# Second attention and routing of a two-layer decoder: one stage of eight units in place of two stages

## The chip, the cores and the metric

The kernel runs on one core of a Trainium2 chip. The metric is the time of one execution on the device in microseconds (us), median of several runs. Five engines work side by side, each through its own queue in order: TensorE (PE: matrix products and turns, with its weight loads shown apart as PEld), VectorE (DVE), ScalarE (ACT), GpSimd (POOL), and SyncE (SP), which here only issues transfers. Everything is in 32-bit floats.

## What is computed

The input has 8 rows of 512 positions with 256 channels. Two layers, each an attention and a feed-forward part, every part behind a normalization and added to its input. The first layer is an ordinary attention with relative positions, and a feed-forward part with GELU. The change touches the second layer:

```python
# attention over the eight ROWS at one position; 16 heads of 16 channels
qkv = x @ Wqkv.T + bqkv
scores = mask + scale * jnp.einsum('bnd,bmd->bnm', q, k)   # n, m: rows
out = softmax(scores) @ v ; x = x + out @ Wproj.T + bproj
# mixture of experts: 32 experts in 4 groups, 4 experts a token
scores = sigmoid(norm(x) @ router_weight.T); sfc = scores + router_bias
# keep the 2 best groups (sum of their two best), then the 4 best experts
x = x + sum_of_chosen(silu(t @ gate) * (t @ up) @ down * weight) + shared_expert(t)
```

The mask lets rows 0 to 3 see rows 0 to 3, and rows 4 to 7 see all eight rows. So the attention mixes rows, never positions: for each position a row has four or eight keys. The experts mix nothing; each token goes to four of them.

## The kernel before

The 4096 tokens are held in on-chip memory as x[0] to x[7], a row each, 128 partitions x 4 tiles x 256 channels (512 positions are 4 tiles of 128). The program has five stages: first attention, first feed-forward, second attention, routing, experts. Everything around the change is ordered by hand: inside `tc.manual_schedule()` the instructions stand in each engine's queue in the order in which the program makes them. No planner moves them.

**Second attention** (class `_L1Attention`, L723 to L985). Its weights come in early (`load`, during the feed-forward). Row 0 is measured and normalized at the end of the feed-forward (L698 to L702). For each row: `measure` and `norm` (DVE's statistics, a power on POOL at L57 for the root, a DVE shift at L751, four ACT instructions at L758), `turn` (8 turns on PE, L799, copies on ACT), `queries` (q and k, L812, evacuated with the bias on ACT, L815), `tokens` (v, L824). Rows 0 to 3 are prepared first; then the rest is prepared while rows 0 to 3 attend. Attention takes four query rows (a group g) at once:

- `multiplied` (L777): q of a row times k of a row, an elementwise product of 128 x 1024; 48 of them. `multiply` deals them to DVE, POOL, DVE in turn, by a counter.
- `summed` (L852): PE adds the channels of a head with a matrix of ones, four query rows beside each other in 32 columns each; `scored` (L869, L870) turns the sums to positions on the partitions.
- `softmax` (L880 to L887): maximum, difference, exponential on ACT (L882), sum, reciprocal, product.
- `weighted` (L777 again): v times its weights, 48 products of 128 x 1024, dealt out in the same way; `gathered` (L904): PE turns and adds them in PSUM; two ACT copies (L916); the bias added to x by POOL (L918).
- `projected` (L927, L935): PE multiplies by Wproj, DVE adds into x.

**Routing** (in `_l1_ffn`, L1083 to L1349), row by row, after the attention. Normalization (`measure`, `norm`), `turn` (L1105, L1108), `logits` (L1115, sigmoid L1119), `copies` (four ACT copies of the normalized rows into the payload, L1098), `hidden` and `gated` (the shared expert, L1266, L1268, L1274), `route` (some 50 small DVE instructions, L1125 to L1178, that choose 4 experts a token), `count`, `take` and `send` (L1184 to L1250: how many tokens each expert has so far, and from that a slot in a table of rows sorted by expert; room for each expert is rounded up to 128 rows). PE's small sums in `count`, `take` and `send` (L1184, L1197, L1198, L1219 to L1221) alternate with DVE's small instructions. Then 16 scatters a row (L1059, POOL, 128 rows of 264 numbers each) carry the payload to DRAM; `pace` issues them two at a time at fixed points of DVE's work, which the scatters wait for. `outputs` and `add_shared` (L1285, L1298) add the shared expert one row later. At the start of the routing SP loads its small weights (L1005 to L1028) and then the weights of all 32 experts in eight transfers of 1536 KB (L1031).

**Experts** (L1350 to L1480): 160 tiles of 128 sorted rows are fetched (`fetch`, after the last 16 scatters), turned, multiplied by their expert's weights (L1385, L1403), and scattered back by POOL (L1059, with the results). `gather`, `add`, `put` fetch the four results of a token, add them and write rows of the output.

A row's PSUM tiles come from pools: the attention's products of q, k, v and turns share two banks, and so do the routing's small sums.

Of the kernel before, what the change touches and what calls it, by code (L numbers as in the profile page):

```python
# [535 lines left out]
class _FFN:  # L536
# [99 lines left out]
    def run(self, rest, after):  # L636

        nc, tc, x, rows = self.nc, self.tc, self.x, self.rows
        with ExitStack() as ctx:
# [43 lines left out]
            with tc.manual_schedule():  # L683
# [5 lines left out]
                for b in range(B):  # L689
                    hT = sb.tile([P, NF, S], F32, tag="hT", name="hT")  # L690
                    for f in range(NF):
# [6 lines left out]
                        if b == B - 1:  # L698
                            if f == 2:
                                after.measure(0)  # L700
                            elif f == 4:
                                after.norm(0)  # L702
                            continue
# [19 lines left out]
class _L1Attention:  # L723

    SEEN = (4, 8)

    def __init__(self, nc, tc, a, x, ident, mhalf, wp):  # L730
        self.nc, self.tc, self.a, self.x, self.ident, self.mhalf, self.wp = nc, tc, a, x, ident, mhalf, wp
        self.stats, self.xl = {}, {}
# [14 lines left out]
    def measure(self, n):  # L747
        nc, wp = self.nc, self.wp
        mv, rstd = _batch_norm_stats(nc, wp, [self.x[n][:, t, :] for t in range(NT)], 1e-5, self.mhalf)
        shift = wp.tile([P, NT], F32, tag="shift", name="shift", bufs=2)  # L750
        nc.vector.scalar_tensor_tensor(shift, mv[:, :, 0], -1.0, rstd, ALU.mult, ALU.mult)  # L751
        self.stats[n] = rstd, shift

    def norm(self, n):
        rstd, shift = self.stats.pop(n)
        xl = self.xl[n] = self.wp.tile([P, NT, H], F32, tag="xl", name="xl", bufs=2)
        for t in range(NT):
            self.nc.scalar.activation(  # L758
                xl[:, t, :], self.x[n][:, t, :], AF.Identity, bias=shift[:, t : t + 1], scale=rstd[:, t : t + 1]
            )  # L760

    def run(self):
        nc, tc, x, ident = self.nc, self.tc, self.x, self.ident
        with ExitStack() as ctx:
            pool = lambda name, bufs, **kw: ctx.enter_context(tc.tile_pool(name=name, bufs=bufs, **kw))
            wp = pool("b_w", 1)
            sb = pool("b_sb", 2)
            ps_q = pool("b_psq", 2, space=PSUM)
            ps_s = pool("b_pss", 2, space=PSUM)
            ps_o = pool("b_pso", 2, space=PSUM)  # L770
            q, k, v = {}, {}, {}
            xlT, prods, sums, sc, values, turned = {}, {}, {}, {}, {}, {}
            engines = [nc.vector, nc.gpsimd, nc.vector]
            count = [0]

            def multiply(out, in0, in1):
                engines[count[0] % 3].tensor_tensor(out, in0, in1, ALU.mult)  # L777
                count[0] += 1

            def bank(name, pool=ps_q, tag="psq"):  # L780
                return pool.tile([P, S], F32, tag=tag, name=name)

            def biases():

                pb = bank("pb")
                for c in range(NK):
                    nc.tensor.matmul(
                        pb[:, :H], self.bcol[:, 4 + c : 5 + c].to_broadcast([P, P]), self.wproj[:, c, :],
                        start=c == 0, stop=c == NK - 1,
                    )  # L790
                nc.vector.tensor_tensor(self.bproj, self.bproj, pb[:, :H], ALU.add)


            def turn(n):
                xlT[n] = sb.tile([P, NK, S], F32, tag="xlT", name="xlT")
                for c in range(NK):
                    pt = bank("pt")
                    for t in range(NT):
                        nc.tensor.transpose(  # L799
                            pt[:, t * P : (t + 1) * P], self.xl[n][:, t, c * P : (c + 1) * P], ident  # L800
                        )
                    nc.scalar.copy(xlT[n][:, c, :], pt)

            def queries(n, c):

                to = (q, k)[c // NK]
                if c % NK == 0:
                    tag = f"q{n % 4}" if c < NK else f"k{n}"
                    to[n] = wp.tile([P, NK, S], F32, tag=tag, name=tag)
                pq = bank("pq")  # L810
                for i in range(NK):
                    nc.tensor.matmul(  # L812
                        pq, self.wqkv[:, i, c * P : (c + 1) * P], xlT[n][:, i, :], start=i == 0, stop=i == NK - 1
                    )
                nc.scalar.activation(to[n][:, c % NK, :], pq, AF.Identity, bias=self.bcol[:, c : c + 1])  # L815

            def tokens(n, half):
                if half == 0:
                    v[n] = wp.tile([P, NT, H], F32, tag=f"v{n}", name=f"v{n}")
                pv = bank("pv")  # L820
                for j in range(2):
                    t = 2 * half + j
                    for i in range(NK):
                        nc.tensor.matmul(  # L824
                            pv[:, j * H : (j + 1) * H],
                            xlT[n][:, i, t * P : (t + 1) * P],
                            self.wqkv[:, i, 2 * H :],
                            start=i == 0,
                            stop=i == NK - 1,
                        )  # L830
                nc.scalar.copy(v[n][:, 2 * half : 2 * half + 2, :].rearrange("p t c -> p (t c)"), pv)

            def row(n):
                ahead = [partial(self.measure, n + 1), partial(self.norm, n + 1)] if n + 1 < B else []
                steps = [partial(turn, n)]
                steps += [partial(queries, n, c) for c in range(4)] + [partial(tokens, n, h) for h in range(2)]
                for i, f in zip((2, 4), ahead):
                    steps.insert(i, f)
                return steps


            def multiplied(g, m):
                prods[g, m] = [sb.tile([P, NK, S], F32, tag="prod", name="prod", bufs=6) for r in range(4)]
                for r, p in enumerate(prods[g, m]):
                    multiply(p, q[4 * g + r], k[m])

            def summed(g, m):
                ps = bank("ps", ps_s, "pss")
                ends = prods.pop((g, m))
                for c in range(NK):  # L850
                    for r, p in enumerate(ends):
                        nc.tensor.matmul(  # L852
                            ps[32 * r : 32 * r + 32, :],
                            self.heads[:, c, :],
                            p[:, c, :],
                            start=c == 0,
                            stop=c == NK - 1,
                            skip_group_check=True,
                        )
# [105 lines left out]
            def beside(main, other):  # L965

                n, done = len(main), 0
                for i, f in enumerate(main):
                    f()
                    upto = (i + 1) * len(other) // n  # L970
                    for f in other[done:upto]:
                        f()
# [642 lines left out]
```

## Time and profile before

| | us |
|---|---|
| median of 3 runs | 2185.62 (2185.58 to 2187.22) |
| the profiled execution, its own time | 2187.77 |
| its span, first to last instruction | 2185.7 |
| first feed-forward ends, attention begins | 1403 |
| attention's last addition into x (L935) begins | 1680.9 |
| last scatter of the routing begins (L1059) | 1897.4 |
| first expert matmul (L1385) | 1904.1 |

Over the whole span PE is busy 2002.9 us (92%), DVE 1395.5 (64%), POOL 1213.7 (56%), ACT 1096.2 (50%), at a mean granted TensorE clock of 0.947. The first two stages hold PE at 90% and more. The rest is not so.

How to read the lines that follow. A line of the table of stretches gives the stretch (us from the span's start), its length, then for each engine its busy time and, after x, its instructions, then the TensorE clock that was granted as a share of full speed, the mean busy share of the DMA engines, and GB/s. A line of waits names the waiting engine, what it waited for with its line, the sum in us, how often, and the longest. A line of the groups has line, engine, operation, output <- inputs, shape, count | busy us in all, mean ns of one | idle time of the engine before them and what ended it. PE's matmuls are pipelined: their mean duration is longer than the busy time that each adds. A 32-bit product of two matrices stands as two instructions in PE's records.

### The profile page before, as it was taken

The numbers are of one execution on the slowest core, as the hardware profiler recorded it, in microseconds if no ns is written. First come the engines' busy times: TensorE is split into PE (matmuls) and PEld (weight loads), VectorE is DVE, ScalarE is ACT, GpSimd is POOL, SyncE is SP. The second block draws the span as 40 slices with busy tenths as digits, with TensorE's granted clock in tenths as the row PEclk, the third lists the DMA queues.
The fourth block names the chain that finished last, engine by engine and source line by source line (L and its number), as shares of the span: only waits on it lengthen the run. The fifth ranks groups of instructions, "written<-read, shape, count | busy, mean of one in ns | idle before, by whom it ended". The sixth has DMA issues, their size and how long they took to land. (4 is left out here: it accounts for less than half of the span.)

```text
span 2185.7 us, 46365 instructions
## 1 busy us (share of the span) xinstructions
PE 2002.9 (92%) x16100; PEld 1464.0 (67%) x16100; DVE 1395.5 (64%) x3664; ACT 1096.2 (50%) x2367; POOL 1213.7 (56%) x1367
## 2 busy tenths in 40 slices
PE   7999999999999999999998999977867888499997
PEld 4777777777777777777775666644536666388886
DVE  3676776767767667676666555344677767356666
ACT  2776676666666666666651222243211545044443
POOL 4666766767667676676753111032546467555554
PEclk7999999999999999999999999998989777699998
DMA  8998898888888988989873444900001622356887
GB/s 273 310 296 276 273 280 267 282 277 274 264 277 275 287 268 270 282 276 288 261 256 91 161 138 129 61 0 1 1 0 54 252 90 95 106 161 207 255 261 257
DMA packets 389061, 444.50 MB, mean 203 GB/s; under 512 B 43232, under 2 KB 368096, under 8 KB 388832
## 3 DMA queue, kind: packets, MB, share of 16 engines
q1 hardware_dynamic: 374048, 402.20, 60.8%
q0 software_dynamic: 13824, 38.29, 4.8%
q8 instruction: 132, 2.16, 0.4%
q10 hardware_dynamic: 960, 1.05, 0.1%
q14 instruction: 97, 0.79, 0.1%
HBM read 239.26 MB, written 202.19 MB: 202 GB/s over the span
## 5 line engine op out<-in xcount | busy, mean ns | idle before, releaser
L389 DVE CUSTOM_DVE_ANT_0 e<-sc,winc 128x512 f32<-128x512 f32 x512 | 333.2, 688 | 297.9 <-PE sc L375 132.5
L391 ACT ACTIVATE e<-e,low 128x512 f32<-128x512 f32 x512 | 365.8, 716 | 115.5 <-DVE low L389 110.4
L316 POOL TENSOR_TENSOR own<-aside,strip 128x512 f32<-128x512 f32 x256 | 268.5, 1049 | 217.2 <-ACT strip L313 200.9
L313 ACT COPY strip<-pa 128x512 f32<-128x512 f32 x512 | 275.3, 591 | 209.0 <-issue 80.1
L363 PE MATMUL sc<-sm,sm 32*128 32x256 f32 (+3 forms) x1792 | 321.3, 438 | 16.7 <-DVE low L389 16.7
L400 DVE COPY et<-et_ps 128x512 f32<-128x512 f32 x512 | 328.5, 683 | 0.2 <-PE et_ps L398 0.2
L306 PE MATMUL pa<-pos,sm 32*128 32x256 f32 x2048 | 299.9, 406 | 1.7 <-ACT sm L290 1.0
L398 PE MATMUL et_ps<-ident,e 128*128 128x128 f32 x2048 | 267.4, 274 | 0.2 <-DVE et L400 0.2
L363 PEld LDWEIGHTS sc<-sm,sm 32*128 32x128 f32 x1792 | 161.8, 184 | 126.3 <-issue 49.4
L398 PEld LDWEIGHTS et_ps<-ident,e 128*128 128x128 f32 x2048 | 233.4, 142 | 0.6 <-ACT e L391 0.5
L343 POOL TENSOR_TENSOR winp<-winp,own 128x256 f32<-128x256 f32 x256 | 186.5, 729 | 74.9 <-DMA winp<-shift 63.5
L1059 POOL DMA_INDIRECT results<-y,r x160 | 156.0, 975 | 124.3 <-ACT y L1405 100.1
L375 PE MATMUL sc<-ident,winp 128*128 128x128 f32 x1280 | 200.1, 285 | 7.9 <-DMA winp<-shift 7.8
L343 POOL TENSOR_TENSOR winc<-winc,own 128x256 f32<-128x256 f32 x256 | 186.7, 729 | 33.8 <-DMA winc<-shift 28.4
L57 POOL TENSOR_TENSOR rstd<-var,mhalf 128x4 f32<-128x4 f32 x40 | 40.8, 1019 | 292.1 <-DVE var L55 267.4
L375 PEld LDWEIGHTS sc<-ident,winp 128*128 128x128 f32 x1280 | 136.4, 141 | 83.1 <-issue 62.6
L306 PEld LDWEIGHTS pa<-pos,sm 32*128 32x128 f32 x2048 | 180.3, 187 | 13.7 <-ACT strip L313 3.6
L1385 PE MATMUL pge<-store,rT 128*128 x640 | 167.9, 385 | 3.0 <-DVE rT L1379 2.8
L1059 POOL DMA_INDIRECT rows<-pay,slot x128 | 128.0, 1000 | 75.2 <-issue 23.8
L410 PE MATMUL ctx_ps<-et,v 128*16 128x128 f32 x4096 | 137.6, 274 | 0.2 <-DVE et L400 0.2
L282 PE MATMUL pq<-xnT,wqk 128*128 128x512 f32 x256 | 127.0, 617 | 4.3 <-DVE xnT L77 4.3
L660 ACT ACTIVATE hT<-ph,b 128x512 f32<-128x512 f32 x64 | 43.9, 687 | 170.0 <-PE ph L657 170.0
(219 smaller groups left out, 3530.8 us busy)
## 6 DMA issues: line engine op xcount, KB each, us to landing
shift<-strip SPq DMA_DIRECT2D x256, 510.0 KB
winp<-shift SPq DMA_DIRECT2D x128, 384.0 KB
winc<-shift SPq DMA_DIRECT2D x128, 384.0 KB
winp<-shift SPq DMA_DIRECT2D x128, 256.0 KB
winc<-shift SPq DMA_DIRECT2D x128, 256.0 KB
rows<-empty SPq DMA_DIRECT2D x8, 2640.0 KB
r<-rows SPq DMA_DIRECT2D x160, 132.0 KB
z<-results SPq DMA_DIRECT2D x32, 512.0 KB
```

What stands on the lines that cost most here:

```text
L306: nc.tensor.matmul(pa[:, t * W : (t + 1) * W], src[rs, i * P : (i + 1) * P], pos[rs, g, :], start=True, stop=True)
L313: nc.scalar.copy(st[:, 2 * j : 2 * j + 2, :].rearrange("p t w -> p (t w)"), pas[j])
L316: nc.gpsimd.tensor_tensor(own, aside.unsqueeze(2).to_broadcast([P, 2, 2, P]), st[:, :, W - 1 : W].rearrange("p (j t) o -> p t j o", t=2).t ...
L343: nc.gpsimd.tensor_tensor(dst, dst, own[:, t], ALU.add)
L363: nc.tensor.matmul(sc[:, c0:c1], s[side_][rs, cut : cut + P], s[2 + side_][rs, c0:c1], start=c0 == 0, stop=False, skip_group_check=True,)
L375: nc.tensor.matmul(sc[:, m * P : (m + 1) * P], wins[n + 2 * (m - i)][1][:, j, (i - m + 1) * P : (i - m + 2) * P], ident, start=False, stop ...
L389: nc.vector.tensor_tensor_reduce(e, sc, wins[n][0][:, j, :], 1.0, -LOW, ALU.add, ALU.min, low)
L391: nc.scalar.activation(e, e, AF.Exp, bias=low, scale=-1.0, accum_out=totals[b, g][:, i, r : r + 1])
L398: nc.tensor.transpose(et_ps[:, ms], e[:, ms], ident)
L400: nc.vector.tensor_copy(et, et_ps)
L1059: ins = nc.gpsimd.indirect_dma_start(to, bass.IndirectOffsetOnAxis(ap=index, axis=0), source, None, bounds_check=last)
L1385: nc.tensor.matmul(pg[:, :H], rT[:, k * P : (k + 1) * P], w[:, k * H : (k + 1) * H], start=k == 0, stop=k == NK - 1)
```

## The change

The two stages become one function, `_l1`. Its unit u is not a row but half of the positions (two tiles of four) of two rows, 2p and 2p+1, with h the half: u = 4h + p (`_halves`). So a unit has as many tokens as a row. Units with p = 0, 1 see four keys, those with p = 2, 3 eight: the order is 4, 4, 8, 8, 4, 4, 8, 8. A unit needs the keys and values only of units of its own half up to its own, or up to the other unit of its pair. All steps are written as events with a time (`at`), sorted by that time, and made in this order; the times only set the order in which each engine's queue is filled. In one period stand: the preparation of unit u+2 (`prepare`), the normalization of unit u+3, the attention of unit u (`attend`) and the routing of unit u-1 (`routed`). The written periods are 40 for a unit of four keys and 48 for one of eight.

Other parts of it: all 96 products go to DVE, none to POOL; a product takes both rows of a unit against one row of keys; the softmax is done for a unit at a time in two parts; `count`, `take`, `send` and `add_shared` are each split in two, so that PE's part and DVE's part stand at different places (`hop`); `gated` and `hidden` are split by halves; the scatters are paced by events and tied to the DVE instruction made last before (`_Recorded`); there is one payload in place of two. In PSUM two banks (`quick`) serve the turns, queries, values, sums, scores, logits and gate, three (`slow`) the rest, one the shared up product, two the turned values. The small weights of the routing are loaded at the start of the stage; the experts' weights behind the attention, into the memory that its pool has left. Statistics and normalization read tiles of two rows. The first unit's shift instruction stands one step after its statistics in the feed-forward. Destinations of results follow the new order of tiles (`tiles` in `_constants`). The output is written in halves of rows.

Cut to its core (new code; `measure2`, `norm2`, `turn2`, `logits`, `route`, `send` keep the arithmetic of the old steps):

```diff
-                engines[count[0] % 3].tensor_tensor(out, in0, in1, ALU.mult)
+        def multiplied(u, m):
+            n, r = of_row(u, m)
+            p = prods[u, m] = ap.tile([P, NK, 2, S // 2], F32, tag="prod", name="prod", bufs=5)
+            two = lambda w: w.rearrange("p c (r s) -> p c r s", r=2)
+            vec.tensor_tensor(
+                p, two(q[u]), two(k[n])[:, :, r, :].unsqueeze(2).to_broadcast([P, NK, 2, S // 2]), ALU.mult
+            )
...
+        def prepare(u, t):
+            for c in range(NK):
+                at(t + 0.6 * c, turn1, u, c)
+            for c in range(2 * NK):
+                at(t + 1.6 + 1.9 * c + (17 if c >= NK and t > 0 else 0), project, u, c)
+            for half in range(2):
+                at(t + 9.3 + 1.9 * half + (17 if t > 0 else 0), tokens, u, half)
+        def normalized(u, t):
+            at(t, inputs.measure, u)
+            at(t + 3.2, inputs.shift, u)
+            at(t + 3.3, inputs.norm, u)
+        def attend(u, t):
+            n = seen(u)
+            for m in range(n):
+                at(t + (2.6 + 1.22 * m if m < 4 else 5.2 + 1.22 * m), multiplied, u, m)
+            for g in range(n // 4):
+                at(t + (7.9, 16.6)[g], summed, u, g)
+                at(t + (9.9, 18.3)[g], scored, u, g)
+            at(t + 16, biased, u)
+            when = (
+                (11.0, 12.5, [14.0, 23.5, 25.6, 28.4]) if n == 4 else (19.7, 25.3, [26.9, 28.1, 30.2, 31.4, 34.4, 35.6, 41.9, 43.1])
+            )
+            at(t + when[0], softmax1, u)
+            at(t + when[1], softmax2, u)
+            for m in range(n):
+                at(t + when[2][m], weighted, u, m)
+                at(t + when[2][m] + 1.4, gathered, u, m)
+            for r in range(2):
+                at(t + when[2][-1] + 3.0 + 0.7 * r, projected, u, r)
+        def routed(u, t, n):
+            at(t + 0.2, measure2, u)
+            at(t + 5.0, norm2, u)
+            at(t + 8.2, turn2, u)
+            at(t + 10.0, logits, u)
+            at(t + 13.4, hidden, u, 0)
+            at(t + 20.0, hidden, u, 1)
+            split = route(u)
+            at(t + 15.3, next, split)
+            at(t + (21.1 if n == 8 else 19.0), next, split, None)
+            late = 3.5 if n == 8 else 0.0
+            hop(count, u, first=t + 23.4 + late / 2, then=t + 25.0 + late)
+            at(t + (19.6 if n == 8 else 18.9), gated, u, 0)
+            hop(take, u, first=t + 26.0 + late, then=t + 27.8 + late)
+            at(t + 29.5 + late, gated, u, 1)
+            for i in range(TOPK):
+                at(t + 24.6 + late + 1.1 * i, copied, u, i)
+            hop(send, u, first=t + 28.0 + late, then=t + 30.5 + late * 1.8)
+            for r in range(2):
+                hop(add_shared, u, r, first=t + 32.6 + late + r, then=t + 36.5 + late * 2 + 0.7 * r)
+            for i in range(8):
+                at(t + 36.0 + late * 1.8 + 2.6 * i, pace)
+        T = [40.0 if seen(u) == 4 else 48.0 for u in range(U)]
+        start = [sum(T[:u]) for u in range(U + 1)]
+        at(-29.0, biases)
+        prepare(0, -28.0)
+        normalized(1, -27.5)
+        prepare(1, -14.0)
+        normalized(2, -13.0)
+        for u in range(U):
+            t = start[u]
+            if u + 2 < U:
+                prepare(u + 2, t + 0.01)
+            if u + 3 < U:
+                normalized(u + 3, t + 7.6)
+            attend(u, t)
+            routed(u, t + T[u], seen(u + 1) if u + 1 < U else 4)
+        events.sort(key=lambda e: e[:2])
         with tc.manual_schedule():
-            first = [f for n in range(4) for f in row(n)]
...
+            while events and events[0][0] < start[U]:
+                events.pop(0)[2]()
+        attention.close()
+        store = keep.tile([P, NE, 3 * H], F32, tag="store", name="store")
+        for e in range(0, NE, 4):
+            nc.sync.dma_start(store[:, e : e + 4, :], a["experts"][e : e + 4].rearrange("e p c -> p e c"))
+        with tc.manual_schedule():
+            for _, _, f in events:
+                f()
+            while waiting:
+                pace()
+            experts()
```

Lines of the code after the change that the prediction names: the head sums `summed` are L952.

## The prediction

> **What bounds the kernel now.** I read the page first, then the busy time by stage, the waits of each stage, and last the rows of single shapes. The profiled execution took 2187.77 us, of which the span is 2185.7; the median of the runs shown is 2185.62, so I sum in the span and carry the difference over to the median. This is the busy time of each engine in five stretches: preparing the first four rows, the attention while rows are still prepared, the attention after that, the routing, and the wait for the last scatters.
>
> ```profile
> core 0: us, PE busy (x) PEld busy (x) DVE busy (x) ACT busy (x) POOL busy (x), PEclk, DMA share, GB/s
> 1403.00:1438.00 35.00, 32.57 (x108) 17.98 (x107) 9.72 (x42) 19.11 (x34) 4.13 (x5) 1.00 0.00 0
> 1438.00:1560.00 122.00, 97.36 (x445) 60.04 (x445) 58.30 (x69) 42.57 (x76) 39.73 (x18) 0.90 0.00 1
> 1560.00:1682.00 122.00, 90.63 (x528) 58.33 (x522) 104.39 (x65) 14.82 (x28) 74.12 (x31) 0.92 0.00 1
> 1682.00:1876.00 194.00, 166.30 (x592) 118.04 (x592) 133.75 (x711) 88.92 (x120) 119.05 (x119) 0.75 0.40 147
> 1876.00:1904.00 28.00, 1.72 (x8) 1.24 (x8) 3.24 (x7) 0.00 (x0) 17.17 (x18) 0.58 0.34 115
> ```
>
> Only these 501 us (1403 to 1904) are touched; what comes before is untouched, and the expert stage behind (282 us, PE busy 266.5) keeps its 160 tiles. See that PE is the busiest engine of the whole stretch (388.6 of 501 us, 78%) but full only at its start, and that in the attention's second half DVE is nearly full (104 of 122) while in the routing PE runs at a granted clock of 0.75. The answers on waits name the chains that leave PE idle in the attention and DVE idle in the routing:
>
> ```profile
> PE ao L904 <- POOL value L777: 27.3, 7, 13.0
> DVE whole L1186 <- PE pc L1184: 26.9, 8, 4.4
> DVE rule L1224 <- PE pk L1221: 14.9, 8, 2.6
> ```
>
> The first is a turn (L904) that stands behind a product on the slow POOL; the others are small results that DVE waits for in a routing with nothing else to do. The instructions by shape, for the attention:
>
> ```profile
> L777 DVE TENSOR_TENSOR value<-v,sc 128x1024 f32<-128x1024 f32 x32 | 58.9, 1866 | 21.4 <-PE ao L904 21.3
> L777 DVE TENSOR_TENSOR prod<-q,k 128x1024 f32<-128x1024 f32 x32 | 58.1, 1870 | 18.9 <-PE ps L852 16.8 <-ACT q L815 2.1
> L777 POOL TENSOR_TENSOR prod<-q,k 128x1024 f32<-128x1024 f32 x16 | 48.8, 3064 | 31.2 <-PE ps L852 31.2
> L927 PE MATMUL po<-wproj,aoT 128*128 128x256 f32 x128 | 30.3, 381 | 0.3 <-ACT aoT L916 0.3
> ```
>
> and the same for the routing's 256-column matmul and for a scatter and a product by tile (ns least, median, most):
>
> ```profile
> L1285 PE MATMUL po<-down,hid 128*128 128x256 f32 x128 | 47.2, 548 | 0.0
> L777 DVE TENSOR_TENSOR prod<-q,k x32: 1210/1218/3381, 1440.2 to 1602.6; 128x1024 f32<-128x1024 f32 x32
> L1059 POOL DMA_INDIRECT rows<-pay,slot x128: 967/973/1376, 1712.0 to 1897.4; - x128
> ```
>
> A product costs DVE 1.22 us alone and 1.87 in the mean beside POOL's products. The same 128 matmuls of 256 columns take 0.237 us each at clock 1.00 and 0.369 in the routing.
>
> **The change, part by part.** *Products.* POOL loses its 32 products and DVE gets all 96: 96 x 1.22 = 117 us, against 64 x 1.87 = 119.5 now. So this is free for DVE if POOL leaves it alone; what remains of POOL's two-input work is the bias (24.7 us in eight now, sixteen halves then). POOL's products took 86 us with 64 x 0.65 = 42 us of DVE's delay beside them, together with the bias 111: 0.37 us of delay per POOL us, so some 9 us in all remain, about 1 per unit. I count them as hidden, because PE is the longer engine.
>
> *Work of one unit.* PE: the attention's 220.6 us fall on 8 preparations and projections and 12 groups of four keys. By the shapes' busy time that is 16.5 per unit and 8.3 per group, which together give 231.6, so I scale by 0.95: 23.6 us for a unit that sees four positions, 31.5 for one that sees eight. The routing's 166.3 become 149.4 at clock 1.00 (the 256-column matmuls 30.3 instead of 47.2), 18.7 a unit. Sum: 42.3 and 50.2. DVE: routing 133.75/8 = 16.7, attention without products (172.4 - 117.0)/8 = 6.9, products 9.8 or 19.5: 33.4 and 43.1. POOL: 16 scatters at 0.97 and 0.30 behind each, two roots of 1.0, the bias 3.1: 26. ACT: 165.4 us and the new table loads below, about 22. So PE is the longest engine in every period, and the plan's own 40 and 48 us per unit cannot be kept: they are below PE's work.
>
> *Waits inside a unit.* I walked the order of the events with these durations. In every unit PE has turned the next input and made its queries by 5.5 us, and stands at the head sums (L952) until DVE has done the statistics of two units' inputs and the four products, at about 8: 2.5 us idle. With four positions the softmax's exponential stands on ACT behind the sigmoid (its logits end at about 14.5), behind the four normalizations (2.1 us) and a table load (1.28): it ends at about 18, DVE's second half of the softmax waits 6 us for it, and PE's first turn of values behind that about 2 to 3. With eight positions this is covered; instead the last two products come after the 5 us of slots on DVE, and PE waits 2 to 3 for them and for ACT's copies before it can project. That makes 47 for four (46 for the sixth unit, which has no normalization beside it) and 53 for eight. The last two units prepare nothing ahead, PE falls to 38, but DVE has 43 - 2.3 = 41 to do and waits for the scores of the second group (3 us), for the counts (2) and for the projection (6): 52.
>
> *Start and end.* The first unit has no routing beside it: PE prepares three rows (3 x 12.1), sums and turns and projects (11.4) and adds the biases (1.0), 49 us, at the 93% busy of the first stretch about 51: it ends at 1454. Then 47 + 53 + 53 + 47 + 46 + 52 + 52 = 350: attention ends at 1804. Behind it the last unit is routed alone. The first routed row now needs from the last addition of the attention (1681.6) to its finished payload (1711.1) 29.5 us, less about 1.5 since only one unit's statistics precede its normalization; then 0.9 to the first scatter, 15 x 1.28, and 6.7 from the last scatter's start (1897.38) to the first expert matmul (1904.12): 28 + 0.9 + 19.2 + 6.7 = 55. First expert matmul at 1859 instead of 1904: **45 us less**.
>
> *Loads.* The eight loads of the experts' weights move behind the attention, since their memory is the attention's, and SP's later fetches stand behind them. Now they are issued from 1686.9 on and the traffic has ebbed by about 1730: some 43 us. The routing of the last unit (55 us) hides them with 12 to spare; uncovered it would be up to 43. The small weights of the routing move ahead, to the start of the stage, with 50 us before their first use. Output halves instead of whole rows: the same bytes on SP, covered by experts. The added shift in the layer before: 0.16 us on DVE, covered.
>
> *Two rules against it.* ACT's table loads rise from 19 to 30, since exponentials now stand among sigmoids and Silus. The row:
>
> ```profile
> 1690.57 1.28 ACT L1119 ACT_TABLE_LOAD   x1
> ```
>
> The Trainium skill ("ScalarE: Activation LUTs", section "Table sets: the hidden batching unit") says to batch activations by table set and gives about 2.7 us a load: 11 x 2.7 = 30 us more on ACT, by the row 11 x 1.28 = 14. I take the row. On an engine with 22 of 47 us to do it costs only where it stands before the exponential, which is in the walk. And the skill ("SBUF — State Buffer", section "Who interferes with whom") says that a DVE instruction with two SBUF inputs and a GpSimd one that reads SBUF block each other for the whole instruction. By that each scatter could wait for a product: 16 x (1.27 + 1.22) = 40, POOL 45 a unit, still under 47, but late for the root that each normalization needs. By the row the worst scatter beside DVE's two-input work took 0.40 more than the median: 16 x 1.67 + 5 = 32. I take the row; the bounds are 0 and, at one such wait before each of two roots in seven units, 17 us.
>
> *PE's clock.* Not shown for this mixture. Lower bound of the cost 0, if it stays at 1.00 as between 1640 and 1680 (PE 86% busy there); upper, if the routing's matmuls stay at 0.75, 7/8 of 16.9 = 15 us. I take 0, as PE is to be about as busy. Hops between engines that my walk leaves out may cost 1 us a unit (7), and it may have overstated PE's waits by the same.
>
> **Rivals.** By PE's share of busy time they line up: PE has 220.6 + 7/8 x 149.4 = 351 us to do before the attention ends, and mine makes it 351/401 = 88%.
> 1. *The waits close up* (22%): the queues run ahead of the plan and PE is 93 to 97% busy, as from 1403 to 1438. 351/0.95 = 370, gain 1904 - (1403 + 370 + 55) = 76: about 2110. For it: the engines' queues now hold other work that is ready. Against: PE's in-order queue stands behind DVE at fixed places.
> 2. *More waits than I walked, the gain mostly given back* (15%): 80 to 82%, as from 1438 to 1560. 351/0.81 = 433, gain 13: about 2173.
> 3. *Slower* (11%): one mechanism, PE's in-order queue behind DVE's products. When a turn of values waits, the next unit's projections and this unit's routing matmuls wait behind it, and their results are what DVE stands at next. PE fell to 74% from 1560 to 1682 by this (27.3 us at L904). At 74%: 351/0.74 = 474, first expert matmul at 1932, 28 later: about 2213. It decides from 351/446 = 78.7% down. Against: there POOL's products of 2 to 3 us were what it waited for, and they are gone.
>
> **How the numbers follow.** My forecast, 45 us off, has 52% with a range of its own of 2120 to 2162. 2185.6 - 45 = 2140.6, rounded to 2140. The range reaches to the middle of the first rival (2104) and into the second (2178). What a measurement can tell from no change is 0.2%, 4.4 us. Faster: 52 + 22 and 11 of the second rival's 15, 0.85; within 0.2%: 0.04; slower: 0.11.
>
> **What would show it.** The first expert matmul at about 1859, the attention's last projection at about 1804; PE 85 to 90% busy between 1454 and 1804 with clock near 1.00; products at 1.22 us on DVE and none on POOL; units of four near 47 us and of eight near 53; DVE's longest wait of a four-position unit the exponential; scatters below 1.4 us. Wrong would be: a clock near 0.75 in the mixture, scatters or roots of 2 us and more, expert weights landing after the last scatter, or an expert stage that is no longer 282 us.

## The result, and the profile after

The changed kernel takes 2160.31 us in the median (2154.41 to 2163.81, 4 runs); the kernel before, measured beside it, 2185.6 (2181.28 to 2187.22). The ratio is 0.9885, with a 95% interval of 0.9858 to 0.9911: 25 us less. The forecast was 2140, 45 less. The profiled execution took 2158.92 us, of which the span is 2157.1.

Busy time by stretch, in the same columns as before: the first unit alone, the seven other units, the tail in which the last unit is routed alone, and the experts.

```profile
core 0: us, PE busy (x) PEld busy (x) DVE busy (x) ACT busy (x) POOL busy (x), PEclk, DMA share, GB/s
1403.00:1457.30 54.30, 44.69 (x180) 27.22 (x179) 20.56 (x44) 24.28 (x42) 5.50 (x5) 0.94 0.06 18
1457.30:1820.80 363.50, 305.26 (x1407) 187.46 (x1405) 275.82 (x807) 145.87 (x215) 147.00 (x125) 0.93 0.11 38
1820.80:1877.70 56.90, 24.11 (x83) 16.01 (x83) 18.63 (x91) 11.18 (x15) 28.35 (x29) 0.65 0.80 303
1877.70:2157.00 279.30, 266.32 (x1436) 221.38 (x1436) 176.75 (x574) 119.48 (x320) 155.82 (x160) 0.98 0.73 226
```

The attention ends at 1820.8 (forecast 1804), and the first expert matmul begins at 1877.7 (forecast 1859, before 1904.1). PE is 84% busy over the seven units, under the 88% of the forecast, at a clock of 0.93.

The kernel before needed 501 us from 1403 to the first expert matmul, the changed one 474.7. The single shapes show how far the costs were read rightly. Each line gives least, median and most in ns, then first and last start:

```profile
L777 DVE TENSOR_TENSOR prod<-q,k x48: 1211/1218/1248, 1412.2 to 1778.2; 128x1024 f32<-128x1024 f32 x48
...
L860 POOL DMA_INDIRECT rows<-pay,slot x128: 967/973/2057, 1502.8 to 1871.1; - x128
...
L1028 POOL TENSOR_TENSOR x<-x,bproj x16: 1257/1273/1283, 1429.9 to 1787.9; 128x512 f32<-128x512 f32 x16
```

All 48 products of queries and keys are on DVE at 1.22 us, as forecast. A scatter that meets one takes up to 2.06 us, but the product doesn't: its longest is 1.25, even where it began while a scatter ran. The other POOL instruction, the bias, is different. Here are two DVE instructions of the softmax and one of the routing:

```profile
L777 DVE TENSOR_TENSOR sc<-sc,top x8: 425/692/3452, 1436.1 to 1789.3; 128x256 f32<-128x256 f32 x4, 128x512 f32<-128x512 f32 x4
...
L777 DVE TENSOR_TENSOR sc<-sc,total x8: 424/692/2600, 1440.3 to 1795.3; 128x256 f32<-128x256 f32 x4, 128x512 f32<-128x512 f32 x4
...
L777 DVE TENSOR_SCALAR rank<-rank x7: 174/177/3107, 1481.7 to 1784.3; 128x16 f32<-128x16 f32 x7
```

An instruction of 0.18 us takes 3.1 in two of seven places. In both, POOL's two halves of the bias (2 x 1.27) run one after the other inside these 3.1 us, and the instruction ends just after them. Such a stall stands in no list of waits: it is booked as DVE's busy time. The lists of waits over the seven units, DVE's and PE's, show the rest:

```profile
DVE x L777 <- PE po L1035: 27.9, 12, 11.2
DVE shift L757 <- POOL rstd L57: 14.9, 4, 4.7
DVE top L777 <- ACT sc L970: 10.3, 4, 4.3
DVE total L777 <- ACT sc L980: 9.2, 3, 3.7
```

```profile
PE ao L1006 <- DVE value L777: 25.5, 9, 6.8
PE ps L953 <- DVE prod L777: 9.4, 7, 4.3
PE pc L1148 <- DVE past L777: 6.2, 2, 4.5
```

The longest wait of the first line, 11.2, belongs to the end of the first unit, so 16.7 of it lie in the seven units. The exponential (L980) was waited for once in each of the three four-key units (3.7, 2.9 and 2.6 us). The root (L57), which stands behind paced scatters on POOL, was late by 1.2 us once and by 4.5 to 4.7 three times, a wait that the forecast had put at 0 of at most 17.

### The profile page after: what moved, and what is told of

It is laid out like the page before. It is cut to its first block, busy times and chain, and to the rows that moved or that the text cites. A ratio compares the mean times of both kernels' runs of the same rounds, so it can differ in the third digit from the quotient of the medians.

```text
span 2157.1 us, 46358 instructions
## 1 busy us (share of the span) xinstructions
PE 1989.8 (92%) x16100; PEld 1439.5 (67%) x16100; DVE 1401.4 (65%) x3716; ACT 1112.0 (52%) x2382; POOL 1140.5 (53%) x1342
## 4 chain that ended last, share of the span: by engine, by line
PE 27%; DVE 10%; issue 4%; POOL 4%; DMA 3%; ACT 2%; POOLq 0%; DVEq 0%; ACTq 0%; SPq 0%
PE po L665 5%; PE pge L1421 4%; PE ph L657 3%; POOL results L860 2%; PE poe L1439 2%; PE pq L916 2%; PE ao L1006 1%; DVE prod L777 1%; PE po L1035 1%; PE pv L928 1%; DVE value L777 1%; PE ps L953 1%; DVE st L52 1%; DVE xn L62 1%; PE ptr L1413 1%
## 5 line engine op out<-in xcount | busy, mean ns | idle before, releaser
L860 POOL DMA_INDIRECT rows<-pay,slot x128 | 141.6, 1106 | 229.5 <-issue 216.3
L57 POOL TENSOR_TENSOR rstd<-var,mhalf 128x4 f32<-128x4 f32 x40 | 44.8, 1121 | 252.6 <-DVE var L55 230.6
```

The source lines that it names most:

```text
L860: ins = nc.gpsimd.indirect_dma_start(to, bass.IndirectOffsetOnAxis(ap=index, axis=0), source, None, bounds_check=last)
```

## The experiments

The start of the stage and the chip's time for the rest vary from execution to execution by some us. So two lengths within the stage are compared, beside the ratios. The first runs from the first copy of a turned input (`xlT`) to the end of the attention's last addition. The second is the **seven units**, from the last addition of unit 0 to the last addition of unit 7 (start to start). Each length is that of one profiled execution. The changed kernel was measured twice: its first two lengths differ by 4.0 and 6.5 us, its seven units (361.7 and 362.9) by 1.2. So differences in the seven units are the ones to go by, and two executions give only a rough figure of their spread.

| run | ratio to before (95%) | from first copy to attention's end | to first expert matmul | seven units |
|---|---|---|---|---|
| before | 1 | (attention 279) | 501.0 | |
| the change | 0.9885 (0.9858 to 0.9911) | 417.2 | 474.1 | 361.7 |
| e5_control (the change again) | 0.990 (0.9884 to 0.9917) | 421.2 | 480.6 | 362.9 |
| e1_no_overlap | 1.0176 (1.0159 to 1.0193) | 302.8 | 550.4 | 243.2 |
| e2_dealt_products | 1.012 (1.0098 to 1.0142) | 480.2 | 537.9 | 419.3 |
| e3_norm_late | 0.9827 (0.981 to 0.9843) | 416.1 | 475.8 | 358.5 |
| e4_norm_only | 0.9844 (0.9826 to 0.9861) | 416.4 | 474.0 | 359.2 |
| e6_no_bias | 0.9851 (0.9831 to 0.9871) | 404.8 | 462.0 | 345.7 |
| e7_rows_by_sp | 0.9828 (0.9808 to 0.9847) | 409.7 | 463.9 | 349.9 |
| e8_one_table | 0.9857 (0.9839 to 0.9874) | 410.2 | 468.2 | 350.9 |
| e9_all_three | 0.9759 (0.9731 to 0.9787) | 391.7 | 445.9 | 333.2 |
| e10_warm | 0.9882 (0.9855 to 0.9909) | 415.0 | 474.7 | 356.4 |
| e11_bias_by_pe | 0.9841 (0.9812 to 0.9869) | 406.9 | 464.0 | 348.1 |
| e12_bias_pe_pace | 0.9859 (0.9835 to 0.9883) | 418.5 | 478.1 | 357.1 |

e1 to e4 ran beside one another on a chip where the kernel before took 2204.68 us, e5 to e8 on one where it took 2190.41, e9 to e11 at 2192.12, e12 at 2196.8. The ratios of different chips differ by more than some of the effects: e3 and e4 have better ratios than the change, but the changed kernel did not run on their chip.

**e1: the same steps without the overlap.**

```diff
-            routed(u, t + T[u], seen(u + 1) if u + 1 < U else 4)
+            routed(u, start[U] + 30.0 * u, 4)
```

> The routing of every unit stands behind the whole attention, one unit each 30 of the written time; units, products on DVE, softmax and split steps stay as in the changed kernel. My theory (the gain is the overlap): units of four fall to about 28 us and of eight to about 36, eight routed units take about 24 each, so the stage is 51 + 228 + 192 + 28 = 500 us and the time about 2187, 27 over the changed kernel. Rival (the gain comes from the unit's shape and from the products all on DVE): it keeps most of the gain, 2170 or less.

The time is 2243.84 us. The stage takes 550.4 us, 50 more than expected: 302.8 of attention (279 were expected) and 247.6 of routing (220). With these units and steps the overlap is worth 550.4 - 474.1 = 76 us. But by themselves, one after the other, they are 49 slower than the old ones (501.0), half of it in the attention (302.8 against 279) and half in the routing. An order that was written for the overlap, and the one payload, may be why; that was not tried. Net, 27 us are left.

**e2: the products dealt to DVE, POOL, DVE again.**

```diff
-            vec.tensor_tensor(
+            multiply(        # DVE, POOL, DVE in turn, in multiplied and weighted
```

> The 96 products are dealt to DVE, GpSimd, DVE in turn again; all else as in the changed kernel. My theory (PE stands behind single products, so a product of 2 to 3 us on GpSimd lengthens the chain, and GpSimd's two-input work blocks DVE's): 2 to 4 us more in each unit, about 2180. Rival (DVE is the engine that sets the period): DVE loses a third of 117 us, the units shorten by 2 to 4 us, about 2140.

The time is 2230.14 us, and the stage takes 64 us more, three times what was expected. The products on POOL now stand in one queue with the paced scatters, and PE stands behind them:

```profile
PE ps L957 <- POOL prod L812: 43.6, 8, 11.1
PE ao L1009 <- POOL value L812: 12.2, 3, 4.3
```

In the kernel before, the same wait for a product on POOL was at most 13.0 us long but came in an attention without scatters. Taking the products off POOL is what makes the overlap pay: with them on POOL the kernel is 1.2% slower than the one before.

**e3 and e4: the next input's normalization later.** In e3 the shift on DVE and the four ACT instructions stand behind the sums' copies and the exponential, at t + 7.9 and t + 8.0; in e4 only the four ACT instructions do.

```diff
-            at(t + 3.2, inputs.shift, u)
-            at(t + 3.3, inputs.norm, u)
+            at(t + (7.9 if t > 0 else 3.2), inputs.shift, u)
+            at(t + (8.0 if t > 0 else 3.3), inputs.norm, u)
```

> Shift (DVE) and normalization (ACT) of the unit three ahead stand 4.7 later in the order: behind the exponential of a unit of four, and behind the root's wait on GpSimd. My theory (these two waits are in the path): 2 us less in each of the two units of four that have it, and up to 4.5 us less in each of the three units where DVE waited for the root, together 8 to 14 us, about 2149. Rival (PE's own work sets the period and hides them): within 3 us of 2160.

> Only the four normalizations on ACT stand 4.7 later; DVE's shift stays where it waits for GpSimd's root. My theory: only the units of four gain, about 2 us in each of two, so about 2156, and DVE's waits of 4.5 us for the root remain. Rival (the root's wait costs nothing, the exponential's does): as good as with the shift moved too.

The times are 2167.15 and 2169.08 us. Up to the attention's end the lengths (416.1 and 416.4) are within what the changed kernel's two executions differ by (417.2 and 421.2); in the seven units 2.5 to 4.4 us are gained (358.5 and 359.2 against 361.7 and 362.9). For e4 that is what was expected: about 2 us in two units of four, with the waits for the root as long as before (14.9). For e3 it is not: of the 8 to 14 us that both waits were to give, 3.2 to 4.4 came, so the root's wait did not stand in the path at its full length. The waits did leave their places, and came back at others. In e3 the root is waited for no more, and the exponential only for 4.4, but:

```profile
DVE top L777 <- ACT sc L970: 19.8, 6, 5.3
...
DVE total L777 <- ACT sc L980: 4.4, 2, 2.6
```

The wait for the scores' copies has grown from 10.3 to 19.8 us.

**e6 to e8: one suspect taken away at a time,** beside the control on the same chip.

```diff
-            at(t + 16, biased, u)                                   (e6)
...
-            ins = nc.gpsimd.indirect_dma_start(...)                 (e7)
+            ins = nc.sync.dma_start(to[s * P : (s + 1) * P, :], source)
...
-            nc.scalar.activation(s, s, AF.Exp, scale=HD**-0.5)      (e8)
+            nc.scalar.activation(s, s, AF.Sigmoid, scale=HD**-0.5)
...
-            nc.scalar.activation(act, pg, AF.Silu)
+            nc.scalar.activation(act, pg, AF.Sigmoid)
```

> The changed kernel itself, so that the three others of this call have it beside them on the same chip. Both theories: from the first copy of a turned input to the first expert matmul 474 us, to the end of the attention's last addition 417, ratio to the kernel before 0.983 to 0.989.

> The projection's bias is left out in this stage (POOL's 16 additions of 1.27 us are gone; the output lacks the bias). Theory A: an addition of two memory operands on POOL blocks DVE beside it (a softmax difference takes 3.45 us instead of 0.69, a rank 0.9 instead of 0.18), about 2 us a unit, and these stand in the unit's path: 8 x 2 = 16 us, so 401 to the attention's end and 458 to the first expert matmul, ratio near 0.977. Rival B: DVE's lengthening is hidden by what PE and ACT do, as the waits for the exponential were: 414 to 418 and 471 to 475, ratio as the control within 0.002.

> The payload's rows are written by SP's plain transfers in order of arrival instead of POOL's indirect scatters (the sorting of the rows is left out; everything that computes the slots stays, and so does the amount written). POOL keeps only roots and biases. Theory A: scatters block DVE's products and delay the roots on POOL (14.9 us of waits at the shift): attention's end 417 less 10 to 18, so about 402; behind it the 16 scatters of the last unit go faster than 1.28 us apart, so the tail of 57 falls to 40 to 48. Rival B: the waits at the root and the slow scatters are hidden during the attention: attention's end at 414 to 418, only the tail falls by 8 to 15. Expert stage 279 in both.

> The exponential and the Silu are replaced by the sigmoid in this stage, so that ACT loads no table inside it (the output is not the reference's); 30 loads of 1.28 us go. Theory A: a load costs only where it stands before a softmax's exponential or a sigmoid that DVE waits for; 2 to 3 such places a unit at 1.28, partly hidden: 5 to 12 us less, 405 to 412 to the attention's end, tail less by 1 to 3. Rival B: hidden like the exponential's wait: 414 to 418. A load at the 2.7 us of the page would give more than 20.

The control took 2168.32 us, and its first two lengths are 4 to 7 us above what was expected of it. The times of e6 to e8 are 2154.97, 2153.46 and 2157.63 us, so 13.4, 14.9 and 10.7 less than the control's; in the seven units they are 17.2, 13.0 and 12.0 less than its 362.9. Each time the result is on the side of Theory A, though up to the attention's end e6 (404.8) and e7 (409.7) gained some us less than it said (401, and 399 to 407); measured from the control's 421.2, they gained what it said. For the bias it can be seen where it went. These are the lines of the whole stretch up to the attention's end, first of the control, then of e6:

```profile
1412.80:1834.00 421.20, 355.15 (x1582) 218.12 (x1582) 293.30 (x837) 170.13 (x257) 151.27 (x129) 0.92 0.10 35
```

```profile
1405.10:1809.90 404.80, 347.04 (x1582) 212.37 (x1582) 277.38 (x834) 170.01 (x257) 131.18 (x113) 0.94 0.10 36
```

DVE issues nearly the same instructions (837 and 834 in the records) and is busy 15.9 us less. That is DVE's lengthening by 20 us of bias on POOL, and the stage is shorter by as much. The root's late arrival is not what changed: DVE waits 14.9 us for it in e6 too. The long instructions are gone:

```profile
L777 DVE TENSOR_TENSOR sc<-sc,top x8: 424/594/693, 1440.0 to 1780.5; 128x256 f32<-128x256 f32 x4, 128x512 f32<-128x512 f32 x4
```

In e7 it is another thing: DVE's busy time in the same stretch is that of the control (292.99 against 293.30), so the scatters don't lengthen DVE's work. What falls is the wait at the root:

```profile
DVE shift L757 <- POOL rstd L57: 4.2, 4, 1.2
```

It was 14.9, and the other 10.7 us are near the 13.0 that the seven units gained. The tail of e7 says nothing of scatters, as the rows then stand on SP behind the eight loads of the experts' weights: 54.2 us, where 40 to 48 were expected. In e8 ACT is busy 33 us less up to the attention's end (25 loads fewer in the records), and the seven units are 12 shorter. ("The 2.7 us of the page" in e8's expectation is the figure for a load that the prediction cites; the more than 20 us that would have followed from it did not come.) The line of e8 for that stretch:

```profile
1407.70:1817.90 410.20, 351.93 (x1582) 215.98 (x1582) 289.88 (x834) 137.04 (x232) 151.35 (x129) 0.93 0.10 35
```

**e9: all three at once.**

> The bias left out, the rows written by SP in order of arrival, and the exponential and the Silu replaced by the sigmoid, all at once (the output is not the reference's). Singly, beside the control, they took 7 to 16 us from the stretch up to the attention's end. Theory A: DVE's lengthening, the late roots and the table loads are separate costs on one chain that alternates between DVE, ACT and PE: they add, about 12 + 9 + 9 = 30, so 387 to 391 from the first turned copy to the attention's end, against 417. Rival B: they all cover the same gaps, and behind them stands PE's in-order queue: no more than the largest, 402 to 406.

The time is 2137.91 us. To the attention's end it is 391.7, 25.5 less than the changed kernel (the control: 29.5); the seven units lose 29.7, where the three losses add up to 42.2. So they are mostly separate costs (Theory A), with some 12 us in common.

**e10: PE kept warm in the last two units.** Dummy products at t + 5.6, 24.9 and 28.2 of each.

```diff
+            if u >= U - 2:
+                for later in (5.6, 24.9, 28.2):
+                    at(t + later, spin)      # 2 x 2 matmuls, 128 x 128 by 512 columns
```

> The changed kernel with dummy products on PE in the last two units, where nothing is prepared ahead, at three places each where PE waits (8 products of 256 rows with 512 columns a place, some 3.8 us each): they only keep PE's clock up. Theory A: the granted clock of 0.69 to 0.85 there stretches the 81 us that PE works in these two units, and it is on the path: clock over 0.9 and 6 to 12 us less, 405 to 411 to the attention's end. Rival B: DVE (85 of 110 us busy) and waits carry these units; PE's clock matters little and the dummies stand in front of real work: 416 to 422.

The time is 2166.57 us. The two last units, in the changed kernel:

```profile
1711.00:1766.50 55.50, 39.85 (x194) 25.89 (x194) 43.45 (x113) 17.24 (x24) 23.86 (x22) 0.85 0.13 46
1766.50:1820.80 54.30, 41.37 (x194) 26.57 (x194) 41.95 (x118) 17.24 (x24) 22.69 (x19) 0.81 0.11 41
```

and with the dummies:

```profile
1715.00:1771.00 56.00, 49.44 (x236) 29.43 (x235) 46.00 (x118) 17.25 (x24) 23.53 (x21) 1.00 0.12 42
1771.00:1825.00 54.00, 48.86 (x233) 28.92 (x232) 42.99 (x118) 17.25 (x24) 24.08 (x22) 1.00 0.14 49
```

The clock is granted in full. From addition to addition these two units take 106.2 us (56.0 and 50.2) against 112.5 in the changed kernel and 112.1 in the control. So some 6 us of the clock's loss were on the path in these two units, the lower end of Theory A. But up to the attention's end it is 415.0, between Theory A's 405 to 411 and Rival B's 416 to 422, and the ratio is no better than the change's own. It is a small gain in the place that was touched, not one that the whole time shows.

**e11: the bias by PE,** complete in its output: a product with ones, into the same PSUM tile, instead of POOL's additions.

```diff
-            at(t + 16, biased, u)
...
             po = slow("po")
+            nc.tensor.matmul(po, some, three.rearrange("p j c -> p (j c)"), start=True, stop=False, skip_group_check=True)
```

> The projection's bias goes into PSUM by one more product on PE for each 512 columns (16-bit, the bias split into three 16-bit pieces that add up to it), in place of POOL's 16 additions; the output stays complete. Theory A: it keeps what leaving the bias out gave (12 to 16 us in the stage) but for the 16 products, for which no row stands here: by the 32-bit matmul of 256 columns at 0.237 us estimated at 0.1 to 0.5 us each, 2 to 8 us on PE, half of it in PE's gaps: 403 to 413 to the attention's end and 460 to 470 to the first expert matmul. Rival B: PE is the longer engine and the products stand at the unit's last step, which DVE waits for: 414 to 420.

The time is 2156.04 us, the seven units 348.1: within 2.4 us of leaving the bias out. Theory A holds. The price that had no row:

```profile
L1051 PE MATMUL po<-three,some x16: 379/379/380, 1461.8 to 1812.3; 128*128 128x512 bf16 x16
```

So most of what the sixteen products take was hidden: the seven units are 2.4 us longer than without any bias. Of the versions that compute everything it has the shortest stage. The intervals of its ratio and the change's still touch (0.9812 to 0.9869 and 0.9858 to 0.9911), so that it beats the changed kernel too rests on the 14 us of the seven units.

**e12: e11 and the scatters out of the roots' way.**

```diff
-                at(t + 36.0 + late * 1.8 + 2.6 * i, pace)
+                at((t + 34.5 + late * 1.8 + 1.3 * i if i < 3 else t + (40 if n == 4 else 48) + 12.0 + 2.4 * (i - 3)), pace)
```

> The bias on PE as in the run before, and the scatters paced so that none stands on POOL ahead of the two roots of a period: three pairs at the end of the unit's routing, the other five from 12 us into the next period on, 2.4 us apart (before: all eight 2.6 us apart from the end of the routing, across the roots). Output complete, same work. Theory A: what the run with the rows written by SP gained (7 to 11 us) was the roots coming in time, as the shift's waits there fell from 14.9 to 4.2 us: here the same, so 406.9 less 7 to 10, 397 to 400 to the attention's end. Rival B: it was the scatters' absence itself (blocked scatters and their descriptors beside DVE), and the root's waits only move, as when the normalization was put later: 404 to 409. A loss, above 410, if the later scatters hold up the copies into the one payload.

The time is 2162.31 us and the seven units 357.1, 9 more than e11: worse. Up to the attention's end it is 418.5, the loss that was named last. And the run tests only in part what it was made for. The second root of a period comes in time, but the first six scatters now stand packed in front of the period's first root, which the routing's shift (here L777) waits for:

```profile
DVE shift L777 <- POOL rstd L57: 7.5, 4, 2.1
...
DVE shift L757 <- POOL rstd L57: 4.2, 4, 1.2
```

Together 11.7, against 2.2 and 14.9 in e11: 5.4 us less of waiting, and yet 9 us more of time. The last scatters of a unit now come late, and ACT's copies into the one payload wait for them (4.5 us in seven waits); whether that is the whole loss was not tried. So here too a root's wait was not worth its length, as Rival B has it, but two things changed at once. Whether the roots alone make up e7's 13 us is therefore open. e3 speaks against the full length, since it took their wait away and gained less than 1 us over e4; but it did so by moving other work later.

## Why the prediction was right in sign and too large in size

**The direction and the place.** The gain is where it was forecast: the stage is shorter and the expert stage is not touched (279.3 us, 2 less than before; forecast unchanged). e1 shows that the overlap itself is the cause (76 us), and e2 that the products off POOL are its condition (64 us). The rival of a kernel that becomes slower had its turning point at PE 78.7% busy; it came to 84%.

**How near it was.** The time lies inside the forecast's own range of 2120 to 2162, but by less than 2 us, and one of its four executions (2163.81) lies beyond. It is nearer to the second rival's 2173, more waits than were walked, than to the forecast's 2140, and so is PE's share: 84%, where the rival had 80 to 82 and the forecast 88.

**The sum, term by term.** From the expected first expert matmul of 1859 to the 1877.7 of the run are 18.7 us:

| term | forecast | measured | difference |
|---|---|---|---|
| end of the first unit | 1454 | about 1459 | +5 |
| three four-key units | 140 (47, 47, 46) | 136.6 (42.8, 47.2, 46.6) | -3.4 |
| four eight-key units | 210 (53, 53, 52, 52) | 225.0 (57.0, 55.5, 58.7, 53.8) | +15.0 |
| seven units together | 350 | 361.7 | +11.7 |
| tail | 55 | 56.9 | +2 |

(The single units are measured between additions, the second of each.) With the experts' 2 us less, the span of 2157.1 is 16 above the forecast. PE's work in the seven units was right in its sum: 303 us were forecast, and PE was busy 304.2. What was too small is its waits: 47 us in the forecast, 57 in the run. The line of the stretch between the two additions:

```profile
1458.40:1820.00 361.60, 304.16 (x1401) 186.52 (x1399) 274.99 (x804) 145.87 (x215) 147.00 (x125) 0.93 0.11 38
```

Two sums of the prediction do not come out by its own terms. An eight-key unit that prepares others is 50.2 us of PE's work, 2.5 of waiting for the first products and 2 to 3 for the last: 55, not 53, which is 4 of the 11.7 us. And the first unit's 48.7 us at 93% are 52.4, not 51.

**The step that failed** is the term "some 9 us in all remain, about 1 per unit. I count them as hidden, because PE is the longer engine". It was wrong twice. The size: leaving the bias out took 15.9 us off DVE's busy time, 0.8 us of delay for each of POOL's 20, where 0.37 was read from POOL's products; the bias meets the short instructions of softmax and routing, and holds up a whole chain, not only a product. And the cover: PE has the more work, but it stands behind DVE's values (25.5 us) at fixed places, so the delay came through in full, 17.2 us of the seven units.

It is the largest failed term that a run measured, not the only one. The late root, taken at 0, was worth up to 13.0 us (e7; e12 leaves its share open). Together these are more than the 11.7 that were missing, so other terms of the walk were too long, and that its sum came so near was in part luck. Without the bias (e6) the seven units take 345.7, only 4 under the forecast, but the four-key units are 10 shorter than forecast (129.6) and the eight-key ones 6 longer (216.2).

**Waits.** The exponential was forecast as a wait of 6 us in each four-key unit and the longest of DVE's there. It came in all three, but at half the size (9.2 us together), and it was the longest only in the first of them. With the normalization moved out of its way (e4) 2.5 to 3.7 us came off. The wait for the scores of the second group in the last two units was forecast at 3 us and took 2.9 in each; one of 4.3 in the sixth unit was not walked.

**The two rules.** For the scatters the row was taken (at most 0.40 us longer), against the Trainium skill ("SBUF — State Buffer", "Who interferes with whom"), by which they block each other for a whole instruction. The longest scatter, 2.06 us, is near the rule's 0.97 + 1.22, but only the scatter was lengthened and not the product. All 128 have a mean of 1.11, so a unit's scatters cost 16 x (1.11 + 0.30) = 22.5 us, under the 40 of the rule and also under the 16 x 1.67 = 27 of the row. But the late root that the prediction drew from the rule was there, within the bounds of 0 to 17: 14.9 us of waits. The rule's own form, a DVE instruction with two inputs held up for a whole one of POOL, was seen at the bias: the softmax's difference of 0.69 us took 3.45. The rank of 0.18, with one input, was held up as well. For table loads the row of 1.28 us was right; e8 shows 12 us on the path for 33 us of ACT, where the forecast counted only the loads ahead of the four-key units' exponential.

**PE's clock.** It was taken as 1.00; it was 0.93, and 0.85 and 0.81 in the last two units, which prepare nothing ahead. That cost some 6 us there (e10), within the bounds of 0 to 15; what the clock cost in the other five (0.89 to 1.00) was not tried.

**The first unit and the tail.** PE was 82% busy until 1457, not 93%: it waited 7.1 us once for a value, which the walk did not have. The experts' loads stayed hidden, as forecast: their traffic ebbs about 1860, some 17 us before the first expert matmul.

## What to carry to other kernels

When two stages are laid beside each other, list for each engine the instructions that will newly meet, and price a meeting by the victim's chain and not by the offender's length: here 20 us of two-operand additions on a POOL that was busy 40% of the time cost 17 us of the seven units, and a small product on PE took their place for 2. "Another engine is the longer one" hides a delay only where that engine does not stand behind the delayed one; read it from its list of waits. And to learn whether a wait is on the path, take its cause away: moving the waiting instruction moved the waits here, and told little.

## What the runs showed of the hardware

- The blocking between POOL and DVE was one-sided by kind in these traces: beside DVE's product of 1.22 us a scatter's issue on POOL grew from 0.97 to as much as 2.06 us, while the product took at most 1.25, also in the 21 cases where it began during a scatter. Beside POOL's addition of two operands, a DVE instruction of 0.18 us took 3.11, and one of 0.69 took 3.45.
- Such a blocked instruction is booked as busy. Without the bias, DVE's busy time was 277 us instead of 293, for the same instructions.
- A 16-bit product of 512 columns showed 0.379 us in PE's records.
- PE's granted clock rose from 0.81 and 0.85 to 1.00 when its busy share in the last two units rose from 72 to 76% to 88 to 90% by dummy work.
